# Mamba scan in a held order: du by DMA, and GpSimd's product with B, in every third group instead of every fourth

## The chip, the cores and the metric

The kernel runs on one core of a Trainium2 chip. The metric is the time of one execution on the device in microseconds; the median of several runs is given, and one further execution was recorded by the hardware profiler.

## What is computed

An image batch of 4 x 96 x 64 x 64 goes through four layers. Layers 0 and 2 are of the kind that the change touches: two Mamba blocks one after the other on the image as a sequence of L = 4096 positions, then a fusion with a global pool and a batch norm. One Mamba block, with DIN = 192 channels and 16 states:

```python
h = layernorm(seq); xs, z = split(h @ in_w)
xc = silu(causal_conv4(xs))
dt, Bm, Cm = split(xc @ xproj_w)                  # 6, 16, 16
delta = softplus(dt @ dt_w + dt_b)
dA  = exp(delta[..., None] * A)                   # L x 192 x 16
dBx = delta[..., None] * Bm[:, :, None, :] * xc[..., None]
# h_t = dA_t * h_{t-1} + dBx_t, along L
hstates = associative_scan(comb, (dA, dBx))[1]
y = (einsum('blds,bls->bld', hstates, Cm) + Dp * xc) * silu(z)
return y @ out_w
```

Layer 1 (a Mamba-2 block in four directions) and layer 3 (a ConvNeXt block) are not touched.

## The kernel before

Two images are worked on together. A *step* is one (pair of images, block, chunk of T = 512 positions): 2 x 2 x 8 = 32 steps in a Mamba layer, 64 in the program. The two images' 384 channels lie in three tiles j of 128 partitions. The scan needs 16 states for each channel, so it spreads 8 channels over 128 partitions (8 channels x 16 states) and handles two such pieces at once (GS = 2, tiles of 128 x 1024): a *group*. A step has 24 groups, g = 8j + 2q + p, with j in 0..2, q in 0..3, p in 0..1.

What a group passes through, with the names used in the profile:

- `load` (L326): `da`, the channels' delta, each row repeated over its 16 states, read by SyncE's DMA queue from a DRAM copy `dd`; two transfers of 256 KB.
- Kind T (product on TensorE): `spread` (L343) makes `bs`, du = delta * xc spread over the states, in PSUM by four matmuls with a selection matrix; `decay` (L111) takes the exponential of `da` in place on ScalarE; VectorE multiplies `bs` by B (L369) and scans `da`, `bs` in two instructions (L374).
- Kind D (by DMA, `g["dma"]`): `load` also fetches `du` from the DRAM copy `dg`, two more transfers; `spread` writes the exponentials into the PSUM tile `bs` instead; GpSimd multiplies `du` by B (`product`, L351); VectorE only scans `bs`, `du` (L374).
- Both kinds: GpSimd multiplies the states by C (`after`, `hc`, L381), ScalarE keeps the last state (`carry`, L384), TensorE sums over the states into `py` (`sums`, L400, and the Dp term L394). After the eighth group of a j, VectorE multiplies `py` by the gate (`close`, L408); `py` has one PSUM bank. `project` and `project_rest` (L416, L418, L424) multiply by `out_w`, ScalarE moves the result out (`keep`, `fuse`).

Beside the groups of a step runs the front of the next step (`mamba_front`): layer norm (L178, L179, L184, L190), in-projection with convolution (L205, L210), z (L215, L220), x-projection (L228, L233), softplus (L269, L287 to L299), and on GpSimd delta and du (L251, L252), which SyncE stores to DRAM (L246). It is advanced by one or two pieces a group (`PACE`).

The order is held: `run` emits, for each n, the stages of several groups, and chains each engine's instructions to that order. At n the engines get: load of group n+5; spread of n+1; decay of n+2; after of n-1; product of n+2; scan of n; close of n-4; pieces of the front; sums of n-3; project of n-5. Every engine works through its own queue in this order. Buffers: eight tiles shared by `da` and `du`, four each of `hs` and `hc`, two of `bs`, two of `xz`.

The kind of each group is fixed in `run`:

## Time and profile before

| | |
|---|---|
| median of 3 runs | 9756.96 us (9746.79 to 9757.15) |
| profiled execution, its own time | 9748.23 us |
| its span from first to last instruction | 9746.5 us |
| PE / PE weight loads busy | 8319.4 us (85%) / 3486.3 us (36%) |
| DVE (VectorE) busy | 8080.8 us (83%) |
| ACT (ScalarE) busy | 5536.2 us (57%) |
| POOL (GpSimd) busy | 6860.0 us (70%) |
| mean granted TensorE clock | 0.927 |
| DMA queue of SyncE | 1519.79 MB, 58.6% of 16 engines' time |

Busy shares are averages over the whole program; the Mamba layers, the Mamba-2 layer and the ConvNeXt layer have different limits. An engine's idle time is put down to the instruction whose signal ended it. TensorE's ends are modelled, so its busy time is not its peak.

### The profile page before, as it was taken

Reading aid. Unit: us, or ns where it says so; the run is one execution under the profiler, and the core shown is the slowest. Engines: PE = TensorE matmul, PEld = TensorE weight load, DVE = VectorE, ACT = ScalarE, POOL = GpSimd, SP = SyncE. Lnnn points to the kernel's source line nnn. Section 1 sums busy time; section 2 is a strip of 40 time slices with the busy share of each in tenths; the row PEclk is TensorE's granted clock in tenths of the full one; section 3 lists DMA queues with packets and bytes.
Section 4 is the critical chain, followed back from the end, with each engine's and each line's share of the span. In section 5 each row is a group of like instructions: output and inputs, shape, how many; then the busy total and the mean of one; then the engine's idle time right before and its main releaser. Section 6 shows DMA issues by size and latency. Waiting matters only on the chain. (4 is left out here: it accounts for less than half of the span.)

```text
span 9746.5 us, 109952 instructions
## 1 busy us (share of the span) xinstructions
PE 8319.4 (85%) x32896; PEld 3486.3 (36%) x32896; DVE 8080.8 (83%) x10870; ACT 5536.2 (57%) x10786; POOL 6860.0 (70%) x4573
## 2 busy tenths in 40 slices
PE   7888888888887998998898999688888888888678
PEld 1222222112123676776766777212222222222122
DVE  7999999999995666666666667699999999999887
ACT  5566666566664455455555545466666666666345
POOL 6888888888885555555555555588888888888511
PEclk8999999999997999999999999799999999999789
DMA  7777787777774222222322222677787877777653
GB/s 187 202 206 204 211 216 206 205 208 201 209 211 128 66 69 85 80 70 82 88 67 77 82 66 61 159 208 195 210 215 206 213 207 197 209 209 203 168 119 84
DMA packets 813856, 1531.94 MB, mean 157 GB/s; under 512 B 126893, under 2 KB 132425, under 8 KB 809802
## 3 DMA queue, kind: packets, MB, share of 16 engines
q1 hardware_dynamic: 810186, 1519.79, 58.6%
q8 instruction: 260, 4.26, 0.2%
q10 hardware_dynamic: 3072, 5.11, 0.1%
q14 instruction: 338, 2.77, 0.1%
HBM read 1229.28 MB, written 148.50 MB: 141 GB/s over the span
## 5 line engine op out<-in xcount | busy, mean ns | idle before, releaser
L381 POOL TENSOR_TENSOR hc<-hs,bc 128x1024 f32<-128x1024 f32 x1536 | 3611.0, 2356 | 742.8 <-DVE hs L374 399.9
L374 DVE TENSOR_TENSOR_SCAN hs<-da,carry,bs 128x512 f32<-128x512 f32 x2016 | 2470.8, 1267 | 119.6 <-DVE bs L369 1.4
L343 PE MATMUL bs<-du,seldu 64*128 64x512 f32 x4608 | 1467.8, 667 | 510.1 <-DVE hs L374 505.6
L400 PE MATMUL py<-hc,selsum 128*32 128x512 f32 x6144 | 1670.7, 651 | 261.5 <-DVE xz L408 180.6
L369 DVE TENSOR_TENSOR bs<-bs,bc 128x1024 f32<-128x1024 f32 x1152 | 1406.3, 1221 | 254.1 <-PE bs L343 233.1
L111 ACT ACTIVATE da<-da,w_a 128x512 f32<-128x512 f32 x2304 | 1517.1, 710 | 0.0
L343 PEld LDWEIGHTS bs<-du,seldu 64*128 64x128 f32 x4608 | 409.9, 193 | 1484.3 <-DVE hs L374 1190.2
L351 POOL TENSOR_TENSOR du<-du,bc 128x1024 f32<-128x1024 f32 x384 | 904.7, 2356 | 50.3 <-DMA du<-dg 50.3
L1032 DVE TENSOR_SCALAR seg<-dr,dac 128x128 f32<-128x128 f32 x1536 | 637.0, 448 | 290.0 <-PE y L1077 287.7
L1048 POOL TENSOR_TENSOR seg<-seg,cb 128x384 f32<-128x384 f32 x512 | 514.9, 1007 | 476.5 <-DVE cb L1047 409.0
L374 DVE TENSOR_TENSOR_SCAN hs<-bs,carry,du 128x512 f32<-128x512 f32 x672 | 819.0, 1260 | 0.0
L205 PE MATMUL pu<-h,w_conv 96*128 96x512 f32 (+3 forms) x2048 | 796.4, 624 | 1.4 <-POOL h L179 1.4
L111 ACT ACTIVATE bs<-da,w_a 128x512 f32<-128x512 f32 x768 | 528.7, 688 | 444.9 <-DVE hs L374 431.8
L983 PE MATMUL front<-pk,sconv 128*128 128x512 f32 x1536 | 753.8, 608 | 25.6 <-ACT z L971 21.7
L400 PEld LDWEIGHTS py<-hc,selsum 128*32 128x32 f32 x6144 | 222.4, 111 | 1504.8 <-issue 924.6
L1087 POOL TENSOR_TENSOR y<-y,xs 128x192 f32<-128x192 f32 x496 | 295.1, 595 | 605.1 <-DVE y L1086 590.1
L1100 ACT ACTIVATE y<-yz 128x192 f32<-128x192 f32 x512 | 186.1, 363 | 906.3 <-DVE yz L1099 905.3
L1052 POOL TENSOR_TENSOR xs<-pre,coef 128x576 f32<-128x576 f32 x512 | 597.9, 1172 | 53.4 <-ACT pre L116 25.3
L994 PE MATMUL front<-sconv,pk 128*128 128x192 f32 x3072 | 572.5, 330 | 57.1 <-DVE pre L999 51.9
L384 ACT COPY carry<-hs 128x2 f32<-128x2 f32 x1344 | 246.7, 184 | 514.2 <-DVE hs L374 513.8
L994 PEld LDWEIGHTS front<-sconv,pk 128*128 128x128 f32 x3072 | 496.7, 190 | 89.6 <-DVE pre L999 78.7
L1077 PEld LDWEIGHTS y<-xs,seg 128*128 128x128 f32 x3072 | 442.9, 206 | 144.2 <-issue 83.9
(229 smaller groups left out, 13743.1 us busy)
## 6 DMA issues: line engine op xcount, KB each, us to landing
da<-dd SPq DMA_DIRECT2D x3072, 256.0 KB
du<-dg SPq DMA_DIRECT2D x768, 256.0 KB
dr<-rows SPq DMA_DIRECT2D x256, 384.0 KB
bc<-rows SPq DMA_DIRECT2D x256, 256.0 KB
dd<-delta SPq DMA_DIRECT2D x192, 256.0 KB
dg<-du SPq DMA_DIRECT2D x192, 256.0 KB
pk<-xn SPq DMA_DIRECT2D x128, 384.0 KB
pk<-xn SPq DMA_DIRECT2D x128, 256.0 KB
```

The lines of the kernel that those rows point to most:

```text
L111: self.last = self.scalar.activation(out, in_, func, **kw)
L205: nc.tensor.matmul(pu[r0:r1], lhsT=wt["conv"][:kk, tap, d0:d1], rhs=h[:kk, b, ds(tap, T)], start=(tap == 0), stop=(tap == 3),)
L343: nc.tensor.matmul(g["bs"][:, i], lhsT=self.sel["du"][rows, g["half"], g["q"]], rhs=g["made"]["du"][rows, g["j"]], start=True, stop=True,)
L351: self.tc.nc.gpsimd.tensor_tensor(g["du"], g["du"], self.b_or_c(g, 0), ALU.mult)
L369: nc.vector.tensor_tensor(dbx, dbx, self.b_or_c(g, 0), ALU.mult)
L374: nc.vector.tensor_tensor_scan(hs[:, i], da[:, i], dbx[:, i], init, ALU.mult, ALU.add)
L381: nc.gpsimd.tensor_tensor(g["hc"], hs, self.b_or_c(g, 1), ALU.mult)
L400: nc.tensor.matmul(py[rows], lhsT=self.sel["sum"][:, g["q"]], rhs=g["hc"][:, i], start=(g["q"] == 0), stop=(g["q"] == NQU - 1),)
L983: nc.tensor.matmul(p, lhsT=self.conv[:, i, DI + q * DST : DI + (q + 1) * DST], rhs=pk[:, i, ds(c * T, T)], start=(i == 0), stop=(i == 2),)
L994: nc.tensor.matmul(p, lhsT=pk[:, i, ds(c * Q, Q)], rhs=self.conv[:, i, :DI], start=(i == 0), stop=(i == 2),)
L1032: nc.vector.tensor_scalar(seg[:, h], g["pair"]["dr"][:, c % 2 * NH + h], made["dac"][:, n0 + h : n0 + h + 1], 0.0, ALU.subtract, ALU.min,)
L1052: nc.gpsimd.tensor_tensor(xs, x.to_broadcast([P, 3, NH, HD]), coef.to_broadcast([P, 3, NH, HD]), ALU.mult)
```

## The change

One expression in `run` decides which groups are of kind D. Before, they are those with q even and p = 1: group numbers 1, 5, 9, 13, 17, 21 of a step, every fourth. After, they are those with g % 3 == 1: 1, 4, 7, 10, 13, 16, 19, 22, every third. Nothing else is changed; the two kinds of group themselves are the same.

```diff
             dict(
                 pair=pair, sub=sub, c=c, wt=wts[sub], made=made[n], j=j, q=q, half=p, quarters=(p, p + 2),
                 first=(q == 0 and p == 0), last=(q == NQU - 1 and p == 1),
-                dma=(q % 2 == 0 and p == 1),
+                dma=((2 * (j * NQU + q) + p) % 3 == 1),
             )
```

## The prediction

> **What bounds the kernel now.** I read the page's groups first, then the busy times by stage, then two timelines. [...] There are 64 steps, in two stages that the trace places at 87 to 3017 us and 6224 to 9151 us: 5857 us, 91.5 us a step. The rest of the program does not use the line that is changed.

> The groups (page, part 5; columns: instruction and tiles, count | busy us, mean ns | idle before, what ended it):

> ```profile
> L381 POOL TENSOR_TENSOR hc<-hs,bc 128x1024 f32<-128x1024 f32 x1536 | 3611.0, 2356 | 742.8 <-DVE hs L374 399.9
> L374 DVE TENSOR_TENSOR_SCAN hs<-da,carry,bs 128x512 f32<-128x512 f32 x2016 | 2470.8, 1267 | 119.6 <-DVE bs L369 1.4
> L343 PE MATMUL bs<-du,seldu 64*128 64x512 f32 x4608 | 1467.8, 667 | 510.1 <-DVE hs L374 505.6
> L369 DVE TENSOR_TENSOR bs<-bs,bc 128x1024 f32<-128x1024 f32 x1152 | 1406.3, 1221 | 254.1 <-PE bs L343 233.1
> L351 POOL TENSOR_TENSOR du<-du,bc 128x1024 f32<-128x1024 f32 x384 | 904.7, 2356 | 50.3 <-DMA du<-dg 50.3
> ```

> VectorE's largest wait is the last number of L369: 233 us for a TensorE product, in 64 steps 3.6 us each. Where it falls decides this case, so I cut one step at VectorE's own instructions: start of group 4, of 14, end of the close (L408) after group 19, start of the next group 0, start of its group 4 (busy us of PE, PEld, DVE, ACT, POOL; then TensorE clock, DMA share, GB/s):

> ```profile
> 1571.91:1606.29 34.38, 34.15 (x118) 8.28 (x120) 32.11 (x30) 25.23 (x50) 28.57 (x13) 1.00 0.78 202
> 1606.29:1631.09 24.80, 16.80 (x54) 3.82 (x52) 23.98 (x25) 16.59 (x29) 23.25 (x14) 0.88 0.88 256
> 1631.09:1646.77 15.68, 15.46 (x42) 3.68 (x42) 12.83 (x13) 8.85 (x19) 13.63 (x7) 0.86 0.80 202
> 1646.77:1661.99 15.22, 11.59 (x39) 3.00 (x38) 14.85 (x16) 7.22 (x15) 13.50 (x8) 1.00 0.68 173
> ```

> Four stretches, two bounds. In the first (groups 4 to 13) TensorE is busy 34.15 of 34.38 us, and VectorE is not. In the second (14 to 19) VectorE is busy 23.98 of 24.80. In the third (20 to 23) TensorE again, 15.46 of 15.68, at a clock of 0.86. In the fourth (0 to 3) VectorE. The timelines say why the third is long (start, duration, instruction, wait):

> ```profile
> 1631.32 1.92 PE L400 MATMUL py<-hc,selsum 128*32 128x512 f32 x4 [3.10 <-DVE xz L408]
> 1633.17 2.02 PE L190 MATMUL pc<-X,center 96*96 96x512 f32 x2
> 1635.12 1.13 PE L400 MATMUL py<-hc,selsum 128*32 128x512 f32 x4
> ...
> 1638.07 1.13 PE L343 MATMUL bs<-du,seldu 64*128 64x512 f32 x4
> ```
> ```profile
> 1634.69 2.31 DVE L374 TENSOR_TENSOR_SCAN hs<-bs,du 128x512 f32<-128x512 f32 x2
> 1639.25 1.23 DVE L369 TENSOR_TENSOR bs<-bs,bc 128x1024 f32<-128x1024 f32 x1 [2.25 <-PE bs L343]
> ```

> The one bank of py is free only after the close, so TensorE stands 3.10 us; then four matmuls take 1.92 us where they take 1.05 elsewhere. In its queue the product of group 22 stands behind sums and projections, starts at 1638.07, and VectorE, through with group 21 (from DMA, hence short) at 1637.0, waits 2.25 us.

> [...]

> **The change part by part.** Groups by DMA are now 1, 5, 9, 13, 17, 21; afterwards 1, 4, 7, 10, 13, 16, 19, 22: two more a step, 128 in all. Removed: 128 VectorE products of 1221 ns, 1.31 to 1.35 us each with the gap to their scans, and 512 matmuls (four run in 1.06 us start to start). Added: 128 GpSimd products of 2356 ns (302 us busy) and 256 loads of 256 KB. If VectorE were the bound everywhere, the gain would be 128 x 1.33 = 170 us. It is not, so each stretch is taken alone.

> *Groups 4 to 13.* TensorE makes a product for 6, 7, 8, 10, 11, 12, 14 today, for 5, 6, 8, 9, 11, 12, 14 afterwards: the same number, in a stretch where it has 0.23 us to spare. VectorE's saving (one group) becomes waiting. The product for group 5 now comes straight after the sums that wait for the close. Counting from the close: sums to 1.2, product to 2.3, ready 2.4; group 4's short scans end at 2.3. So 0.1 is lost there, then about 1.2 before group 6 and 1.0 before group 8, all inside TensorE's 34.4. ScalarE's exponentials of group 7 stand behind its copy of xz, which waits for TensorE's L424, and may come 0.6 late, before the wait for group 8 and hidden by it. I take +0.2 us (0 to +0.3).

> *Groups 14 to 19.* VectorE is the bound, and groups 16 and 19 replace 17: one product less, **-1.3 us**. TensorE's 8 us of idling cover the rest.

> *Groups 20 to 23.* TensorE makes the products of 21 and 23 instead of 22 and 23. After the close: sums 1.0, product 21 1.06, pc 1.0, sums 1.0, the projection 1.95, pc 1.03, sums 1.0, L424 with product 23 1.5, latencies 0.2: group 23 can start at 9.75 at full clock. VectorE needs 3.7 + 3.7 + 2.35 = 9.75. Half clock as today adds 0.9 + 1.0: 11.65, and with 3.6 for group 23 the stretch is 15.25 against 15.68: **-0.4 us**. With the clock back at once it is about 13.7 (GpSimd, below, costs 0.3): -2.0. With product 21 at half clock too (+0.95) it is 16.2: +0.5. TensorE's idling before the close gets longer (it loses the product of 19, and stands some 5 us), so I stay near today's clock.

> *Groups 0 to 3.* Group 1 stays; group 4's product leaves TensorE's queue here, where it idles: 0.

> *GpSimd.* 78.8 us of the 89.6 us step are busy; two products make it 83.5. The tight place: from group 15's hc at about 1613.6 it has five hc and two du products (7 x 2.32 from start to start) and three pairs delta, du (2.55 each): 23.9 us, so du of group 22 is ready at 1637.5, and VectorE reaches it at 1629.8 + 7.4 = 1637.2: 0.3 us, under TensorE's delay for group 23. Behind the products queue the hc, 2.3 us later; today they run up to 3 us late without holding TensorE, and hs has four buffers.

> *DMA, SP, ScalarE.* In the second stretch (share 0.88, 256 GB/s) 0.52 MB more take 2.0 us and fill it. Loads are issued five groups ahead and used two or three later (some 9 us), so they land in time: 0, at most 0.3. With eight tiles, a load waits for the scan six groups back; today for one six or seven back. SP issues four more loads of 0.585 us a step, in about 44 us of 90. ScalarE's exponentials keep their number (688 into PSUM, 710 into SBUF): 0.

> Sum: +0.2 - 1.3 - 0.4 = **-1.5 us a step**, x 64 = -96. The profiled execution took 9748.2 (span 9746.5); 9748.2 - 96 = **9652**. The median stands 9 us above that execution, within the spread of the runs; I do not add it.

> **The rivals.**
> 1. *Slower: half clock in the saturated stretch.* Without the product of group 4 TensorE idles about 2.6 us, not 1.14, before the sums that wait for the close after group 3. If the clock falls there, the first stretch begins at half speed; 1.9 us is its price in the timeline above, and TensorE has no slack to pay it. -1.5 + 1.9 = +0.4 a step: 9774; with the third stretch at +0.5, 9831. It decides from four steps in five. [...] Against: a wait of 2.34 us at group 1 mostly left the clock whole. Chance 0.17, at about 9790.
> 2. *GpSimd becomes the bound.* If du of groups 19 and 22 come 1.5 us later than in my count (a delta late, an hc behind a wait), VectorE waits for them and the gain is gone: 9748. Against: 6 us a step remain free. 0.14.
> 3. *The clock comes back early* in the third stretch: +0.2 - 1.3 - 2.0 = -3.1 a step, 9550. 0.12.
> 4. *The change does nothing*: excluded but for an error; the rule picks 8 of 24 groups. 0.02.

> **How the numbers follow.** My forecast has 0.55, its own range 9585 to 9720. Bounds of all parts give 9537 (-3.3 a step) to 9831; 8 times in 10: 9560 to 9790. About 0.2% (20 us) is what a measurement of this kernel can tell from no change. Faster: 0.53 of the forecast, 0.12 of rival 3, 0.03 of rival 2: 0.68. Slower: 0.13 of rival 1, 0.06 of rival 2: 0.19. The rest 0.13.

> **What would show it.** Right: L369 x1024, L351 x512, L343 x4096; groups 14 to 19 shorter by 1.3 us; groups 4 to 13 still 34.4, with VectorE's waits at L369 grown there; the 2.25 us wait gone from group 22, a smaller one before 23. Wrong: clock below 1.00 in groups 4 to 13 (rival 1), scans waiting for POOL du (rival 2), ScalarE or GpSimd waiting for DMA da or du (the transfers).

## The result, and the profile after

The changed kernel takes 9702.33 us (median of 5 runs, 9690.77 to 9719.46) against 9753.9 us (5 runs, 9746.79 to 9757.15): ratio 0.9949, 95% interval 0.9934 to 0.9963. It is faster by 52 us; I had forecast 9652, which is 102 under this median. The time lies in the range that I gave, but the gain is half of what I forecast. The profiled execution took 9696.58 us with a span of 9694.6, against 9746.5.

The groups of the page after that answer to those shown of before (instruction and tiles, count | busy us, mean ns | idle before, what ended it):

```profile
L381 POOL TENSOR_TENSOR hc<-hs,bc 128x1024 f32<-128x1024 f32 x1536 | 3607.7, 2357 | 393.3 <-DVE hs L374 376.3
L374 DVE TENSOR_TENSOR_SCAN hs<-da,carry,bs 128x512 f32<-128x512 f32 x1792 | 2195.7, 1267 | 99.9 <-DVE bs L369 2.4
L343 PE MATMUL bs<-du,seldu 64*128 64x512 f32 x4096 | 1465.1, 743 | 718.7 <-DVE hs L374 718.7
L369 DVE TENSOR_TENSOR bs<-bs,bc 128x1024 f32<-128x1024 f32 x1024 | 1246.7, 1218 | 317.1 <-PE bs L343 314.3
L351 POOL TENSOR_TENSOR du<-du,bc 128x1024 f32<-128x1024 f32 x512 | 1206.9, 2357 | 49.9 <-DMA du<-dg 49.9
...
L374 DVE TENSOR_TENSOR_SCAN hs<-bs,carry,du 128x512 f32<-128x512 f32 x896 | 1094.0, 1262 | 70.9 <-issue 69.4
```

The counts are as expected. That more work on GpSimd would not slow VectorE was an assumption of mine; an instruction of either changed by 3 ns at most in these runs (GpSimd's products 2357 ns, before 2356; the scans 1267 and 1262, before 1267 and 1260; L369 1218, before 1221). Two numbers tell of the loss. L369 is issued 128 times less and yet waits 314 us for TensorE, 81 more than before. And L343, the same instruction, now takes 743 ns on average where it took 667: TensorE was more often at half clock (its mean granted clock over the execution is 0.913, before 0.927).

The step of before that the prediction shows is the first of a block: its scans take no carried state and are shorter (2.33 us a pair against 2.45), and so are its stretches. A step as most are, its groups 4 to 13, 14 to 19 and 20 to 23:

```profile
1388.61:1423.18 34.57, 34.34 (x118) 8.30 (x120) 33.12 (x30) 25.17 (x49) 28.47 (x13) 1.00 0.77 202
1423.18:1448.67 25.49, 16.79 (x54) 3.64 (x50) 24.67 (x25) 16.80 (x29) 23.92 (x14) 0.91 0.88 245
1448.67:1465.22 16.55, 16.31 (x42) 3.68 (x42) 13.33 (x13) 9.75 (x22) 13.01 (x7) 0.83 0.74 203
```

One step of the changed kernel, cut in the same way (start of group 4, of 14, of 20, of the next 0, of its group 4; busy us of PE, PEld, DVE, ACT, POOL, then clock, DMA share, GB/s), and as a last row the first stretch of another step:

```profile
1288.34:1324.76 36.42, 36.19 (x120) 8.44 (x120) 31.78 (x28) 21.52 (x42) 30.15 (x14) 0.95 0.78 201
1324.76:1348.86 24.10, 13.60 (x50) 3.23 (x46) 23.45 (x25) 17.88 (x32) 23.46 (x14) 0.91 0.89 253
1348.86:1365.28 16.42, 16.19 (x42) 3.92 (x42) 13.41 (x12) 9.93 (x22) 16.42 (x8) 0.82 0.94 250
1365.28:1380.50 15.22, 10.45 (x35) 2.70 (x34) 14.85 (x16) 9.48 (x19) 13.40 (x8) 1.00 0.79 196
1926.56:1961.53 34.97, 34.97 (x122) 8.27 (x120) 31.77 (x28) 20.42 (x38) 29.91 (x13) 1.00 0.77 193
```

The second stretch is 24.10 us, 1.39 less than before, close to the 1.3 worked out. The first is 36.42 us at a clock of 0.95 in one step and 34.97 at 1.00 in the other, with TensorE busy nearly all the time in both. The timelines of the slow one, TensorE's, then VectorE's, and a line of ScalarE's (start, duration, instruction, wait):

```profile
1288.57 1.05 PE L400 MATMUL py<-hc,selsum 128*32 128x512 f32 x4 [2.56 <-DVE xz L408]
1289.55 1.78 PE L343 MATMUL bs<-du,seldu 64*128 64x512 f32 x4
1291.26 1.97 PE L205 MATMUL pu<-h,w_conv 96*64 96x512 f32 x4
1293.17 1.10 PE L400 MATMUL py<-hc,selsum 128*32 128x512 f32 x4
...
1297.11 1.08 PE L205 MATMUL pu<-h,w_conv 96*64 96x512 f32 x4
```
```profile
1291.38 1.23 DVE L369 TENSOR_TENSOR bs<-bs,bc 128x1024 f32<-128x1024 f32 x1 [0.59 <-PE bs L343]
...
1297.22 1.23 DVE L369 TENSOR_TENSOR bs<-bs,bc 128x1024 f32<-128x1024 f32 x1 [2.05 <-PE bs L343]
...
1302.32 2.46 DVE L374 TENSOR_TENSOR_SCAN hs<-bs,carry,du 128x512 f32<-128x512 f32 x2 [1.29 <-issue]
```
```profile
1300.24 0.59 ACT L210 COPY xz<-pu 128x512 f32<-128x512 f32 x1 [12.00 <-PE po L424]
```

TensorE stands 2.56 us before the sums that wait for the close after group 3. The sums still run at full clock (1.05 us); then the product of group 5 takes 1.78 and the four matmuls L205 take 1.97 where they take 1.08 at 1297.11. The granted clock is at half from 1289.89 to 1293.31. VectorE waits for TensorE at groups 5 and 6. Group 7's scans wait 1.29 us for their exponentials, which stand in ScalarE's queue behind its copy of xz, and that behind TensorE's L424, as I had said; this wait is there without half clock too (1.29 us at 1939.09 in the step from 1926.56). The half clock is rival 1 of the prediction, in most steps (42 of 58, below).

To count it, I took from the traces VectorE's first instruction of groups 4, 14, 20 and 0 in every step, and the records of the granted clock, in stretches of 3.41 us and multiples of it. Means over 58 inner steps (each stage without its first and its last two steps; "half" counts steps with more than 3 us of half clock in that stretch). The last column counts the groups 0 to 3 that follow. The rows below the second are the experiments.

| kernel | groups 4-13 | 14-19 | 20-23 | 0-3 | step, us | half in 4-13 | half in 0-3 |
|---|---|---|---|---|---|---|---|
| before | 34.74 | 25.45 | 16.42 | 15.19 | 91.81 | 0 | 9 |
| changed | 35.97 | 24.02 | 16.20 | 15.21 | 91.41 | 42 | 11 |
| head | 35.67 | 25.44 | 15.96 | 15.19 | 92.25 | 31 | 29 |
| tail | 35.16 | 24.03 | 15.94 | 15.29 | 90.42 | 0 | 50 |
| warm4 | 34.84 | 24.03 | 16.35 | 16.14 | 91.36 | 0 | 46 |
| pad | 35.95 | 25.35 | 15.64 | 15.18 | 92.11 | 42 | 18 |
| five | 33.91 | 24.03 | 15.70 | 15.20 | 88.84 | 1 | 11 |
| fill_before | 34.56 | 25.45 | 14.44 | 15.18 | 89.62 | 0 | 0 |
| fill | 34.79 | 24.20 | 14.17 | 15.19 | 88.35 | 0 | 0 |
| late_fill | 35.09 | 24.30 | 14.00 | 15.25 | 88.64 | 9 | 51 |
| fill_five | 33.74 | 24.30 | 13.82 | 15.18 | 87.04 | 0 | 0 |

In the changed kernel the 42 steps with half clock in the first stretch take 36.43 us there, the other 16 take 34.77: the price of one occurrence is 1.66 us.

This tells the steps of the changed kernel apart. In 46 of the 58, TensorE waits over 2 us before the close after group 3 (2.56 in the median), and in 42 of these half clock follows; the four that are spared are first steps of a block, with at most 1.76 us of the wait in one window. In the other 12, groups 0 to 3 already ran at half clock, TensorE came late to the close and waited 0.32 us there on average. The step from 1926.56 is one of these.

### The profile page after: what moved, and what is told of

Same layout as the page of the kernel before. It is cut to its first block, busy times and chain, and to the rows that moved or that the text cites. A ratio compares the mean times of both kernels' runs of the same rounds, so it can differ in the third digit from the quotient of the medians.

```text
span 9694.6 us, 109728 instructions
## 1 busy us (share of the span) xinstructions
PE 8189.0 (84%) x32384; PEld 3465.0 (36%) x32384; DVE 7920.0 (82%) x10742; ACT 5522.4 (57%) x10786; POOL 7153.5 (74%) x4701
## 5 line engine op out<-in xcount | busy, mean ns | idle before, releaser
L381 POOL TENSOR_TENSOR hc<-hs,bc 128x1024 f32<-128x1024 f32 x1536 | 3607.7, 2357 | 393.3 <-DVE hs L374 376.3
L374 DVE TENSOR_TENSOR_SCAN hs<-da,carry,bs 128x512 f32<-128x512 f32 x1792 | 2195.7, 1267 | 99.9 <-DVE bs L369 2.4
L343 PE MATMUL bs<-du,seldu 64*128 64x512 f32 x4096 | 1465.1, 743 | 718.7 <-DVE hs L374 718.7
L400 PE MATMUL py<-hc,selsum 128*32 128x512 f32 x6144 | 1584.7, 641 | 201.2 <-DVE xz L408 195.9
L369 DVE TENSOR_TENSOR bs<-bs,bc 128x1024 f32<-128x1024 f32 x1024 | 1246.7, 1218 | 317.1 <-PE bs L343 314.3
L111 ACT ACTIVATE da<-da,w_a 128x512 f32<-128x512 f32 x2048 | 1348.9, 709 | 0.0
L351 POOL TENSOR_TENSOR du<-du,bc 128x1024 f32<-128x1024 f32 x512 | 1206.9, 2357 | 49.9 <-DMA du<-dg 49.9
L374 DVE TENSOR_TENSOR_SCAN hs<-bs,carry,du 128x512 f32<-128x512 f32 x896 | 1094.0, 1262 | 70.9 <-issue 69.4
L111 ACT ACTIVATE bs<-da,w_a 128x512 f32<-128x512 f32 x1024 | 705.4, 689 | 665.5 <-DVE hs L374 648.8
L343 PEld LDWEIGHTS bs<-du,seldu 64*128 64x128 f32 x4096 | 397.9, 210 | 1642.5 <-DVE hs L374 1208.6
L205 PE MATMUL pu<-h,w_conv 96*128 96x512 f32 (+3 forms) x2048 | 827.4, 657 | 1.4 <-POOL h L179 1.4
L400 PEld LDWEIGHTS py<-hc,selsum 128*32 128x32 f32 x6144 | 213.8, 111 | 1441.0 <-issue 760.6
L210 ACT COPY xz<-pu 128x512 f32<-128x512 f32 x192 | 110.7, 577 | 713.4 <-PE po L424 686.1
```

What stands on the lines that cost most here:

```text
L111: self.last = self.scalar.activation(out, in_, func, **kw)
L205: nc.tensor.matmul(pu[r0:r1], lhsT=wt["conv"][:kk, tap, d0:d1], rhs=h[:kk, b, ds(tap, T)], start=(tap == 0), stop=(tap == 3),)
L343: nc.tensor.matmul(g["bs"][:, i], lhsT=self.sel["du"][rows, g["half"], g["q"]], rhs=g["made"]["du"][rows, g["j"]], start=True, stop=True,)
L351: self.tc.nc.gpsimd.tensor_tensor(g["du"], g["du"], self.b_or_c(g, 0), ALU.mult)
L369: nc.vector.tensor_tensor(dbx, dbx, self.b_or_c(g, 0), ALU.mult)
L374: nc.vector.tensor_tensor_scan(hs[:, i], da[:, i], dbx[:, i], init, ALU.mult, ALU.add)
```

## The experiments

**The kernel before, once more.** Is the whole difference of the two profiled executions due to the change?

> The kernel before once more, with a profile of its own: how much of the 52 us between the two profiled executions lies where the change does nothing. The scan stages took 2930 and 2926 us before and 2906 and 2912 after (-38 us); the Mamba-2 layer between them took 3207 before and 3194 after (-13 us), though its instructions are the same. If that is scatter between executions, this profile shows the middle part anywhere between about 3190 and 3210 us and scan stages within 3 us of 2930 and 2926. If the change reaches into the Mamba-2 layer, it is again at 3207 within 2 us.

9761.17 us, a single execution. Its middle part, counted as in the expectation, takes 3214 us (before 3207, changed 3194), a little over the band that I had set; its scan stages take 2933 and 2929 us, 3 more than before in each. The other kernels, none of which touches the middle part, have it between 3192 and 3221. So the 13 us by which the two profiles differ there lie within its scatter, and the scan stages account for 38. The difference of the two medians, 52, can hold such scatter too.

**warm4.** The product of group 4 is made on TensorE again, for nothing:

```diff
         if g["dma"]:
+            if 8 * g["j"] + 2 * g["q"] + g["half"] in (4,):
+                for i in range(GS):
+                    rows = ds(HALFP * i, HALFP)
+                    nc.tensor.matmul(
+                        g["bs"][:, i], lhsT=self.sel["du"][rows, g["half"], g["q"]],
+                        rhs=g["made"]["du"][rows, g["j"]], start=True, stop=True,
+                    )
             self.exps(g, g["bs"])
```

> The changed kernel with one addition: for group 4 TensorE makes the product with the selection matrix as it did before, into the bs tile that ScalarE then overwrites with the exponentials. It computes nothing that is used; it fills TensorE's wait before the close after group 3. Clock theory: the loss in groups 4 to 13 (35.85 us a step on average, against 34.73 before) is a half-clock window of 3.4 us that starts about 1.5 us after group 4 in most steps, because TensorE idles there; with the filling the window is gone, the stretch takes 34.4 to 35.0 us in nearly all steps, and the time falls by 45 to 90 us to about 9635. Order theory: the loss is the new order of the queues (product of group 5 straight behind the sums, exponentials of group 7 behind L424) and the clock only goes along; then the time stays within 15 us of 9702, since all that order is unchanged.

9711.77 us (9695.12 to 9724.91), ratio to before 0.9953 (0.9941 to 0.9966): no better than the change alone. By the time alone, the forecast of the order theory came true and that of the clock theory did not. Yet in the first stretch it did what the clock theory says, with the order of the queues otherwise unchanged: no half clock, 34.84 us. The loss came out elsewhere. The fourth and first rows of one of its steps (columns as above), and TensorE's timeline at groups 1 and 2 of it:

```profile
1292.01:1326.91 34.90, 34.90 (x121) 8.27 (x120) 31.79 (x27) 24.10 (x48) 28.79 (x13) 1.00 0.83 211
...
1367.60:1384.17 16.57, 14.14 (x39) 3.66 (x38) 15.04 (x15) 6.91 (x14) 14.64 (x9) 0.79 0.67 178
```
```profile
1371.45 2.08 PE L350 MATMUL bs<-du,seldu 64*128 64x512 f32 x4 [2.43 <-DVE hs L381]
1373.46 2.07 PE L401 MATMUL py<-xz,w_dd 128*128 128x512 f32 x2
```

(L350 is L343, L401 is L394 of the other listings.) The stretch that I had set at 0 takes 16.57 us instead of 15.22, because TensorE, having waited 2.43 us, runs it at 0.79. In the table half clock there went from 11 steps to 46. It also costs more there: groups 0 to 13 take 51.21 us in the steps with it and 50.06 in those without. In the changed kernel they take 50.22 with it; there TensorE has a wait of 2.53 us before the close in which to catch up, in warm4 one of 1.34. Filling one wait moved the loss to another one and gained nothing.

**head and tail.** The two halves of the change.

```diff
-                dma=((2 * (j * NQU + q) + p) % 3 == 1),
+                dma=(8 * j + 2 * q + p in (1, 4, 7, 10, 13, 17, 21)),      # head
+                dma=(8 * j + 2 * q + p in (1, 5, 9, 13, 16, 19, 22)),      # tail
```

> Groups by DMA 1, 5, 9, 13, 16, 19, 22: the kernel before in groups 0 to 13, the changed one in 14 to 23. If the parts of a step add up, groups 14 to 19 save 1.4 us and groups 20 to 23 0.2 us a step, as between the two profiles, and groups 4 to 13 lose nothing: 64 x 1.6 = 100 us, about 9650. If the half-clock windows only move to another place when a step gets shorter (a step of 92.16 us is 27 windows of 3.41 us), less than half of that is left: 9700 or more.

9654.18 us, ratio 0.9894 (0.9881 to 0.9908), 103 us under the kernel before, measured alongside: the saving of groups 14 to 19 is there in full (24.03 us) and is kept. Groups 4 to 13 take 35.16 us, more than before, without any half clock in them: after groups 0 to 3 at half clock, in 50 steps, they take 35.25, in the other eight 34.59.

> Groups by DMA 1, 4, 7, 10, 13, 17, 21: the changed kernel in groups 0 to 13, the kernel before in 14 to 23; the other half of the change. The tail half alone gave 9654 (about -98 us), both halves 9702. Clock theory: this half brings the idling before the close after group 3 and a half-clock window in the first stretch, 36.4 us instead of 34.6 in most steps, and saves nothing elsewhere: 40 to 100 us slower than before, 9795 to 9850. If the halves act only together (the windows fall in place by the step's length), the time stays within 20 us of before.

9771.63 us, ratio 1.0023 (1.0015 to 1.0031): 21 us slower, less than the 40 us I had set as the least; the half clock is in the first stretch in 31 of 58 steps, the ones in which TensorE waits over 2 us before the close; in the other 27, groups 0 to 3 ran at half clock. So the half in groups 14 to 23 is the gain, and that in groups 0 to 13 gives part of it back. The sum of the two, -82 us, is more than the whole change gives: the windows fall differently in each kernel.

**five.** Group 5 goes by DMA in the place of group 4.

```diff
-                dma=((2 * (j * NQU + q) + p) % 3 == 1),
+                dma=(8 * j + 2 * q + p in (1, 5, 7, 10, 13, 16, 19, 22)),
```

> Groups by DMA 1, 5, 7, 10, 13, 16, 19, 22: the changed kernel with group 5 in the place of group 4. Group 4's product is back on TensorE ahead of the close after group 3, and group 5's leaves the stretch in which TensorE is the bound. Clock theory: the idling before the close is again about 1.2 us, no half-clock window in groups 4 to 13, and one product less in a stretch bound by TensorE: about 33.3 us against 35.85, in all 2.5 us a step less than the changed kernel, about 9540. Order theory: group 7's exponentials still stand behind L424 and two groups by DMA close together tighten the eight tiles for da and du; 1 us or less a step is won, 9640 to 9690.

9553.73 us, ratio 0.979 (0.9777 to 0.9804): 149 us less than the changed kernel, from one group. Half clock in the first stretch in 1 step of 58, the stretch 33.91 us, with one product less to make in it. I had reckoned with 33.3. Two things change here at once, the clock and the number of products in the stretch; fill_five below parts them.

**pad.** One VectorE instruction more a step. In 22 of its 58 inner steps the changed kernel lies within 0.1 us of 92.16 = 27 x 3.413; do steps lock to the windows? (The 27 of 62 steps in the expectation should be 22.)

```diff
             nc.vector.tensor_tensor_scan(hs[:, i], da[:, i], dbx[:, i], init, ALU.mult, ALU.add)
+            if i == 1 and 8 * j + 2 * g["q"] + g["half"] == 15:
+                nc.vector.tensor_tensor_scan(
+                    hs[:, i], da[:, i], dbx[:, i], init, ALU.mult, ALU.add
+                )
```

> The changed kernel with one VectorE instruction more a step: the second scan of group 15 is issued twice, with the same inputs and output (1.25 us, in the stretch where VectorE is the bound). Locking theory: a step's length is pulled to 27 windows of TensorE's clock (27 x 3.413 = 92.16 us, where 27 of the 62 inner steps of the changed kernel lie within 0.1 us): what a step saves moves the windows against its work until a half-clock window costs as much. Then most of the added 1.25 us is swallowed: the locked steps stay at 92.1 to 92.2 with the half-clock window shifted, and the time rises by less than 35 us, to 9700 to 9735. Additive theory: the clock's losses are what they are, and the instruction adds 62 x 1.25 = 78 us: 9780.

9763.97 us, ratio 1.001 (1.0003 to 1.0016): 62 us more than the changed kernel, closer to the 78 of the additive theory than to the 35 of the other. The second stretch grew by 1.33 us and the third fell by 0.56. A part is swallowed, but the steps aren't held at 27 windows: 3 of 58 lie there. In this form the theory falls. That 32 of 58 steps of warm4 lie there stays unexplained.

**fill, fill_before, fill_five, late_fill.** TensorE's long waits are filled, in the changed kernel, the kernel before and "five"; in late_fill, the changed kernel again, those of groups 15 to 20 alone.

```diff
+        times = {1: 1, 4: 1, 16: 1, 18: 3, 19: 2, 20: 2}.get(8 * g["j"] + 2 * g["q"] + g["half"], 0 if g["dma"] else 1)
+        for i in [i for _ in range(times) for i in range(GS)]:
+            rows = ds(HALFP * i, HALFP)
+            nc.tensor.matmul(
+                g["bs"][:, i], lhsT=self.sel["du"][rows, g["half"], g["q"]],
+                rhs=g["made"]["du"][rows, g["j"]], start=True, stop=True,
+            )
         if g["dma"]:
             self.exps(g, g["bs"])
             g["terms"] = g["bs"], g["du"]
             return
-        for i in range(GS):
...
```

This is fill. The dictionary, group number to how often its product is made, is {1: 1, 17: 1, 18: 2, 19: 2, 20: 2} in fill_before, {1: 1, 16: 1, 18: 3, 19: 2, 20: 2} in fill_five and {16: 1, 18: 3, 19: 2, 20: 2} in late_fill. Where a group goes by DMA, ScalarE overwrites what TensorE made.

> The changed kernel with TensorE's waits filled: it makes products with the selection matrix that nobody uses for groups 1, 4, 16 (once) and 19 (twice) into bs tiles that are overwritten, and makes that of group 18 three times and of 20 twice, with the same result. Clock theory: without long waits no half-clock window is granted, the first stretch takes 34.6 us, the second 24.0, the third about 14, the fourth 15.2: 88 us a step against 91.2, about 9510, clock above 0.97 in the scan stages. Against it: the added matmuls stand in TensorE's queue and delay what waits behind them, or the clock falls somewhere else again, as with the filling of group 4 alone (9712); then 9690 or more.

9526.55 us (9515.62 to 9537.09), ratio 0.9764 (0.9751 to 0.9777), with 2048 matmuls more than the changed kernel.

> The kernel before with TensorE's waits filled in the same manner: unused products for groups 1 and 17, and those of 18, 19, 20 made twice. Beside the filled changed kernel it gives what the change is worth when the clock stays up. Clock theory: the third stretch loses its 2 us, about 89.5 us a step and 9620; and the filled changed kernel is 1.5 to 2 us a step better (95 to 130 us), which is what I had forecast for the change. If filled and unfilled differ by less than 20 us, the half clock isn't what makes the third stretch long.

9617.46 us (9612.53 to 9632.44), ratio 0.986 (0.9847 to 0.9873). One step of each, fill and then fill_before:

```profile
1250.29:1285.12 34.83, 34.60 (x120) 8.30 (x120) 31.73 (x28) 22.62 (x45) 30.29 (x14) 1.00 0.85 214
1285.12:1309.22 24.10, 19.93 (x74) 5.31 (x70) 23.45 (x24) 16.94 (x32) 23.45 (x14) 0.97 0.92 239
1309.22:1323.73 14.51, 14.27 (x42) 3.56 (x42) 13.30 (x12) 10.83 (x22) 14.51 (x8) 0.94 1.05 280
1323.73:1338.96 15.23, 13.61 (x43) 3.43 (x42) 14.86 (x16) 8.50 (x17) 15.23 (x8) 1.00 0.79 214
```
```profile
1266.25:1300.82 34.57, 34.34 (x118) 8.30 (x120) 33.12 (x29) 25.18 (x49) 28.45 (x13) 1.00 0.81 201
1300.82:1326.32 25.50, 20.24 (x70) 5.17 (x66) 24.68 (x26) 16.80 (x29) 23.93 (x14) 0.93 0.86 249
1326.32:1340.24 13.92, 13.69 (x42) 3.44 (x42) 13.30 (x12) 9.74 (x23) 13.03 (x7) 1.00 0.95 239
1340.24:1355.46 15.22, 13.58 (x43) 3.43 (x42) 14.85 (x15) 7.33 (x15) 13.52 (x8) 1.00 0.73 187
```

The first stretch has a clock of 1.00 in both, and there the change costs 0.26 us in these steps, 0.23 in the means: my +0.2. The second stretch gains 1.40 here, 1.25 in the means. Half clock isn't gone entirely: groups 14 to 23 have 2.9 us of it a step in fill and 3.3 in fill_before, where the kernels without filling have 12.7 and 10.2. GpSimd (the fifth busy time) has no pause in the third stretch of fill, 14.51 of 14.51 us, as it has none in that of the changed kernel: it is close to being the bound there. Between the two filled kernels the change is worth 9526.55 - 9617.46 = -91 us (64 times the difference of the steps in the table is -81), where I had forecast -96. The first two parts of the forecast are borne out by this, the third is not: it was made for a stretch at half clock, so that its -0.4 and the -0.27 here are of different things. And the filling alone takes 135 us from the kernel before (9752.67, measured alongside).

> The filled changed kernel without the filling for groups 1 and 4: only the waits of groups 15 to 20 are filled. If the wait before the close after group 3 alone brings the half clock into the first stretch, it is back there: 36.4 us in most steps, up to 9620. If the windows fall there only because the longer step drifts through them, a step of 88 us mostly misses it: 9530 to 9560 as with all waits filled (9527).

9555.47 us, ratio 0.9798 (0.9785 to 0.9811): half clock in the first stretch in 9 of 58 steps, not in most. Not because the half clock misses the wait: mostly the wait itself is missing. Two steps, each with its groups 0 to 3 and 4 to 13, and TensorE's sums at the close of each:

```profile
969.30:984.68 15.38, 12.88 (x35) 3.33 (x34) 14.96 (x15) 9.48 (x19) 15.38 (x9) 0.78 0.89 238
984.68:1019.67 34.99, 34.99 (x122) 8.28 (x120) 31.79 (x29) 21.52 (x42) 30.26 (x14) 1.00 0.84 205
437.96:453.17 15.21, 10.37 (x35) 2.70 (x34) 14.84 (x15) 9.48 (x19) 15.21 (x9) 1.00 0.81 199
453.17:489.60 36.43, 36.20 (x120) 8.59 (x120) 31.78 (x28) 20.43 (x38) 30.98 (x14) 0.95 0.73 191
```
```profile
985.06 1.05 PE L401 MATMUL py<-hc,selsum 128*32 128x512 f32 x4
...
453.40 1.62 PE L401 MATMUL py<-hc,selsum 128*32 128x512 f32 x4 [2.56 <-DVE xz L409]
```

In 49 of the 58 steps groups 0 to 3 run at half clock (0.78 in the first of these two); TensorE comes late to the close, waits 0.55 us there on average, and groups 4 to 13 have full clock. In the nine others it waits 2.52 us on average, and half clock follows in all nine. Over the changed kernel, head, pad and late_fill together, 124 of 128 waits of over 2 us before the close brought half clock into the first stretch, and none of the 104 steps with groups 0 to 3 at half clock had it there. Half clock in groups 0 to 3 is the cheaper one: groups 0 to 13 together take 50.11 us in the 49 steps and 51.57 in the nine (49.97 in fill).

> Groups by DMA 1, 5, 7, 10, 13, 16, 19, 22 with TensorE's waits filled (unused products for groups 1, 16 and 19, group 18's made three times, 20's twice). Clock theory: first stretch 33.3 to 33.8 us, second 24.0, third about 14, fourth 15.2: 86.8 us a step against 88.8 without the filling (9554), about 9430. If the filling is itself in the way, 9540 or more.

9444.7 us (9428.65 to 9461.83), ratio 0.968 (0.9666 to 0.9694): the best of the versions, 3.2% under the kernel before. Beside fill, with no half clock in groups 4 to 13 in either, the one product less in that stretch is worth 34.79 - 33.74 = 1.05 us a step there, which is what a product takes of TensorE at full clock (its four matmuls 1.06 from start to start).

## Why the prediction missed by half

- **Groups 4 to 13, +0.2 us (0 to +0.3): the step that failed.** It is +1.23 (35.97 - 34.74). What I gave away as rival 1, at 0.17, happened in 42 of 58 steps at 1.66 us each (my price: 1.9): 42/58 x 1.66 = 1.20, less by 0.03 than what is to be explained. The wait that I forecast for it, 2.6 us, was right (2.56). My reason against it was that a wait of 2.34 us at group 1 mostly left the clock whole. It did so because it lay across the border of two windows of the grid of 3.413 us, in 49 of 58 steps; nothing in the new kernel promised the same for the new wait. The half clock that I had seen came after a wait of 3.10 us; that a shorter one would mostly be spared was my estimate. In groups 0 to 3 of all kernels idling of some 1.77 us within one window was enough.
- **Within that stretch:** the order of TensorE's queue was right in the sum: between the filled kernels, without half clock, it grows by 0.23. In its parts it was not. The exponentials of group 7 come 1.29 us late, not 0.6, and the wait of 1.0 that was to hide this, before group 8, isn't there. That the two errors cancel is luck.
- **Groups 14 to 19, -1.3:** -1.43. VectorE was the bound, and stayed it (busy 23.45 of 24.10 us in the step shown).
- **Groups 20 to 23, -0.4:** -0.22, half of it (clock 0.82 in the step shown, 0.83 before). As forecast, the wait at group 22 is gone and one of 2.17 us stands before group 23.
- **Groups 0 to 3, 0:** +0.02. In warm4 the same stretch cost 0.95 more than before, so its 0 was not safe.
- **GpSimd, DMA, SP:** the page shows no wait of ScalarE or GpSimd for da or du beyond the 49.9 us at the start of the stages, and L369's waits are for TensorE. In the trace du of group 22 is ready 0.47 us before its scan on average over the inner steps, and GpSimd has no pause in the third stretch of the step shown. Rival 2 didn't happen, but it is close.
- **The sum:** -1.5 forecast, -0.40 measured in the inner steps, -26 us in 64 of them, -38 us in the stages from first to last scan. With rival 1 in every step it would be +1.66 - 1.43 - 0.22 + 0.03 = +0.04, no gain at all; it came in nearly three steps of four. The chance that I gave it was the mistake, more than its price.

That half clock is the cause of the loss in groups 4 to 13 is shown by its count and price in the changed kernel, by warm4, in which that stretch gets its time back, and by the filled kernels, in which the change gives 91 us. That filling one wait only moves it is shown by warm4. When the wait before the close came, it brought half clock in 124 of 128 cases; in the 104 steps of the same kernels whose groups 0 to 3 ran at half clock there was none behind it. What stays open is what sets the place of the steps on the grid, so that the wait at group 1 brings half clock in 9 of 58 steps in one kernel and in about 50 in another; a lock to 27 windows, as the simple answer, fell with pad.

## What to carry to other kernels

A change that takes work from an engine which waits elsewhere can cost clock: here half clock followed 42 of the 46 waits of over 2 us before the close. Before crediting TensorE's idle time as cover, list every wait in a period and lay it over the grid on which the trace's granted clock changes (3.413 us here); in groups 0 to 3 of these traces some 1.77 us of idling within one window was enough. Price the half clock behind each such wait where the following stretch is bound by TensorE (1.66 us here). Count how many instructions each bound stretch keeps, not how many the kernel loses: moving group 5 instead of group 4 was worth 149 us, the product and the clock together. And where such waits recur, matmuls that nobody uses, put ahead of the wait, can gain more than the change itself: here 135 us of the kernel before with all the long waits filled, and nothing in warm4 with one.

## What was not expected of the hardware

- A wait of 2.56 us brought half clock, and in the step shown it began only when TensorE was at work again: the first four matmuls after the wait ran in 1.05 us, the next in 1.78.
- In the windows of 3.413 us that were at full clock, half clock followed all 887 in which TensorE was busy less than 40% of the time and one of 13812 with 55% or more. A wait of some 2.45 us in groups 0 to 3 (medians 2.46 before, 2.43 changed) brought it or not by how it lay across two windows: in 9 and 11 of 58 steps.
- The same four matmuls of a product take 1.06 us from start to start at full clock and 2.01 at half (warm4, at 1371.45). One stretch of half clock of 3.41 us cost the changed kernel 1.66 us where TensorE was the bound; where half clock fell into groups 0 to 3 of late_fill (3.41 or 6.83 us of it), groups 0 to 13 took only 0.14 us more than in fill.
- Parts of the program that are the same in all kernels (the Mamba-2 layer) took 3192 to 3221 us in the profiled executions: the spread of 29 us is 0.3% of the whole program, more than the 0.2% that I had set as what can be told from no change.
